# Edge softmax of a graph-attention layer: the row term added to the mask before the turn, on one Trainium2 core

## The chip, the cores and the metric

The kernel runs on one core of one Trainium2 chip. The metric is the device time of one execution in microseconds. The engines are called by the names that the profile uses: PE is TensorE (matrix products; PEld is its weight load), DVE is VectorE, ACT is ScalarE, POOL is GpSimd, SP is SyncE, which issues most of the transfers.

## The reference, cut to what matters

There are 128 graphs of 128 nodes with 512 features each. Two layers follow each other; both have the form "layer norm of x plus a graph layer of x". The first layer is masked attention with 8 heads. The second, which the change touches, is a graph attention with one head:

```python
Wh = h @ W                              # [128 graphs, 128 nodes, 512]
s_i = Wh @ a1 ; s_j = Wh @ a2           # one number for each node
e = leaky(s_i[:, :, None] + s_j[:, None, :])      # leaky(x) = x if x >= 0 else 0.2 x
e = where(adj > 0, e, -9e15)
attention = softmax(e, axis=1)          # over i
h_prime = leaky(einsum('bij,bjf->bif', attention, Wh))
```

The softmax runs over i, the first index, and the product sums over j. So the kernel wants the scores as [j, i]: j on the partitions, i along the free axis, where a reduction can run. The mask comes from memory as adj[i, j], with i on the partitions, the other way round. Something has to be turned.

## The kernel before, in words

All 128 graphs go through one core. The main loop runs over t, one graph a round; a round holds the pieces of several graphs at different stages. Graph t has its attention scores and its softmax (class Softmax); a pair of graphs around t - 3 has the output projection of the first layer (LayerZero); a pair around t - 6 has the product with W of the second layer (LayerOne), and graph t - 7 has the edge softmax (class Edge). The query, key and value projections are made for groups of four graphs and are cut into steps that the rounds consume. Hence the loop has a period of four rounds. Large products are made with seven block products in place of eight (Strassen's scheme); their partial results lie in PSUM banks named st_y, st_w, st_x (projections) and p_y, p_w, p_x (pairs of graphs), and ScalarE and VectorE copy or add them out.

The order of the instructions on every engine is written out by hand: no scheduler moves them. In the loop it is the order of the statements of the body. The last rounds, from END = 124 on, are not a loop but a list of pieces, PLAN (from L1151), in which e0 to e10 are the edge softmaxes of the last eleven graphs; e4.turn is the method turn of the fourth after e0, and so on. The list is walked once and each piece is issued in its turn on its engines.

The names and lines that matter:

- mask_float (L479) turns the loaded adj into bf16 (tile mf, nine buffers), and mask (L484) makes it 0 where there is an edge and -1e30 where there is none. The same tile serves the first layer's softmax and, some rounds later, the edge softmax.
- WH[b] is the result of LayerOne: 2 x 257 columns. Column 256 of the first half holds s_i, column 256 of the second half holds s_j, because the weights w1 have been given that column at the start.
- Edge.turn (L781) makes two products on TensorE into one bank, p_e. L784 turns the column s_i, spread over 128 columns, so that it stands as a row on all partitions; L785 multiplies the mask by a bf16 identity, which turns the mask.
- Edge.add (L794) adds s_j, a bias of each partition, on ScalarE and leaves PSUM (tile e).
- Edge.maxima (L798) makes the leaky ReLU on VectorE (L800), adds the turned mask from the bank (L802), and reduces to the negative maximum (L804).
- Edge.exp, divide, product, copy and residual follow: exponential on ScalarE (L808), division on VectorE (L812, L813), the product with Wh on TensorE (L818, bank p_h), the copy to tile z on ScalarE (L824), and then leaky ReLU, residual and layer norm.

In the loop the turn stands in the early part of a round, after the scores of graph t and one step of the projections, and the product with its copy stands at the end of the round, before the first layer's product with the values (L588, bank p_oT) and its copies (L602). In the loop ScalarE's and VectorE's instructions for the edge softmax lie between the exponentials (L540) and the divisions (L554) of the first layer's softmax. In the tail the layer norm of a graph ends with an activation (L649), and the bias bo is put into the banks p_y and p_w by ScalarE (L456).

The PSUM pool "mm" has five banks, which lg, p_y, p_w, p_x, p_e, p_h and p_oT use one after the other.

Of the kernel before, what the change touches and what calls it, by code (L numbers as in the profile page):

```python
# [9 lines left out]
BF16 = mybir.dt.bfloat16  # L10
I32 = mybir.dt.int32
AF = mybir.ActivationFunctionType
ALU = mybir.AluOpType
# [6 lines left out]
ALPHA = 0.2  # L20
# [4 lines left out]
def kernel(  # L25
# [69 lines left out]
    small = ctx.enter_context(tc.tile_pool(name="small", bufs=3))  # L95
# [4 lines left out]
    def psum(name):  # L100
        return ps_mm.tile([P, D], F32, name=name, tag="mm")


    ident = const.tile([P, P], F32, name="ident")
    make_identity(nc, ident)
    ident_b = const.tile([P, P], BF16, name="ident_b")
    nc.vector.tensor_copy(ident_b, ident)
    mhalf = const.tile([P, 1], F32, name="mhalf")
    nc.gpsimd.memset(mhalf, -0.5)

# [109 lines left out]
    X, XT, XS, Q, K, V, MF, OT, X1T, X1, WH = ({} for _ in range(11))  # L220
# [266 lines left out]
    class Softmax:  # L487
# [45 lines left out]
        def maxima(self):  # L533
            self.add(0)
            self.add(1)
            self.reduce()
# [231 lines left out]
    class Edge:  # L768
# [8 lines left out]
        def tile(self, name, shape, pool, bufs):  # L777
            home = self.homes.get(name)
            return home(shape) if home else pool.tile(shape, F32, name=name, bufs=bufs)

        def turn(self):  # L781
            self.s = WH[self.b][:, :, HALF : HALF + 1]
            self.p = psum("p_e").rearrange("p (c k) -> p c k", c=NC)
            nc.tensor.transpose(self.p[:, 0, :], self.s[:, 0, :].to_broadcast([P, P]), ident)  # L784
            nc.tensor.matmul(  # L785
                self.p[:, 1, :],
                MF.pop(self.b),
                ident_b,
                start=False,
                stop=True,  # L790
                skip_group_check=True,
            )

        def add(self):  # L794
            self.e = self.tile("e", [P, P], small, 1)
            nc.scalar.activation(self.e, self.p[:, 0, :], AF.Identity, bias=self.s[:, 1, :])

        def maxima(self):  # L798
            e = self.e
            nc.vector.scalar_tensor_tensor(e, e, ALPHA, e, op0=ALU.mult, op1=ALU.max)  # L800
            self.att = self.tile("att", [P, P], small, 2)
            nc.vector.tensor_add(self.att, self.p[:, 1, :], e)  # L802
            self.nmax = small.tile([P, 1], F32, name="nmax1", bufs=4)
            nc.vector.tensor_reduce(self.nmax, self.att, AX.X, ALU.max, negate=True)  # L804

# [39 lines left out]
    def on(b):  # L845
        return 0 <= b < B
# [14 lines left out]
    none = Nothing()  # L861
# [7 lines left out]

    zero = {}  # L870
    chores = []
    sm = fin = edge = none

    def x_turns(t):
        if t < 0:
# [58 lines left out]
    END = B - GROUP  # L934
    for t in range(-3, END):
# [29 lines left out]
        last, sm = sm, Softmax(t) if on(t) else none  # L965
# [6 lines left out]
        if t < 3:  # L972
            sm.maxima()
            group(2)
            if on(t - 2):
                load_residual(t - 2)
            if t == 0 and on(GROUP):
                sum_x(1)()
            sm.exp(0, 1, 2, 3)
            last.transpose()  # L980
            group()
            sm.reciprocals(0)
            sm.exp(4, 5, 6, 7)
            sm.reciprocals(1)
            sm.divide(0, 1, 2)
            group()
            last.attend()
            sm.divide(3, 4)
            last.copy()
            if t % 2 == 0 and t > 0:  # L990
                last.sum(0, 1, 2, 3)
            sm.divide(5, 6, 7)
            if on(t + 1):
                mask_float(t + 1)
        else:
            sm.maxima()
            group()
            edge = Edge(t - 7) if on(t - 7) else none
            edge.turn()
            edge.add()  # L1000
            fin.residual()
            if on(t - 2):
                load_residual(t - 2)
            edge.maxima()
            fin.stats()
            fin.rstd()
            x1_sums()
# [12 lines left out]
            fin.apply()  # L1020
            fin.store()
            sm.exp(7)
            edge.divide()
            pair()
            sm.reciprocals(1)
            sm.divide(0, 1, 2, 3)
            group()
            sm.divide(4, 5)
            pair()
            sm.divide(6, 7)  # L1030
            if on(t + 1):
                mask_float(t + 1)
            group()
# [8 lines left out]
        if t % 2 == 0 and on(t - 4):  # L1042
# [2 lines left out]
            layer.transpose(1)  # L1045
            sums.append(layer)
        group(21 if t % GROUP == 0 else 1)
        fin = edge
        fin.product()
        fin.copy()  # L1050
# [98 lines left out]
    for n in range(6):  # L1149
# [7 lines left out]
        el.rstd b0.p2 b0.t2 al.transpose.0 s0.divide.0.1 b0.p7 al.sum.0 b0.c11 s0.divide.6.7  # L1157
        b1.p1 al.sum.1 s1.exp.6.7 s0.store al.sum.2 b0.t3 s1.reciprocals.1 s1.exp.0.1 b0.p4
        b0.c22 al.sum.3 s1.divide.4.5 b0.p3 b0.c21 s0.fetch s1.divide.6.7 s2.scores b0.c12 v.t3
        e0.turn s1.exp.2.3 v.c22 v.p4 m2.cast s1.reciprocals.0 e0.add m2.mask s2.add.0  # L1160
        s1.divide.2.3 v.p3 s2.add.1 s1.divide.0.1 b1.t0 s2.reduce s1.store v.c21 b1.p6 el.apply
        v.c12 s2.exp.2.3 el.store s3.scores e0.maxima s2.exp.6.7 s1.fetch sl.attend e0.exp
        s2.exp.4.5 e0.divide e1.turn b1.p5 s0.transpose sl.copy e0.product m3.cast
        s2.reciprocals.1 sl.sum.0 e1.add m3.mask b1.p2 s3.add.0 s2.divide.6.7 sl.sum.1
        s1.transpose s2.divide.4.5 a0.by a0.p1 sl.sum.2 b1.t2 e0.copy sl.sum.3 b1.p7 b1.c11 a0.t0
        s3.add.1 s2.exp.0.1 a0.p6 s3.reduce b1.t3 s0.attend a0.t2 e0.residual s3.exp.0.1 a0.p7
        s3.exp.6.7 a0.bw a0.p5 b1.c22 x2.x a0.t3 s2.reciprocals.0 e1.maxima s3.exp.2.3 a0.p4
        s2.divide.0.1 a0.c22 b1.p3 e1.exp s3.reciprocals.0 s2.divide.2.3 a0.c21 a0.p3 e1.divide
        s3.divide.0.1 s2.store a0.stats.1 e1.product s3.divide.2.3 b1.c12 a0.rstd.1 s3.exp.4.5
        s1.attend e0.stats e1.copy e3.turn s3.reciprocals.1 e0.rstd b1.p4 s0.copy e1.residual  # L1170
        s2.fetch s1.copy a0.p2 e1.stats x3.x s3.divide.6.7 a0.c11 s1.sum.0 a0.c12 s3.divide.4.5
        s1.sum.1 e3.add s3.store a0.stats.0 s1.sum.2 e0.apply a1.by a1.p1 b1.c21 e1.rstd e0.store
        e3.maxima a0.apply.1 e2.turn a1.p2 a1.t0 a0.store.1 s2.transpose e3.exp a0.rstd.0 a1.p6
        e2.add s3.fetch e1.apply e2.maxima a1.bw a1.p5 s1.sum.3 a1.t2 a0.apply.0 e3.divide a1.p7
        e1.store e2.exp a1.c11 a0.fetch.1 s2.attend e2.divide a1.t3 a1.c22 a1.p4 s2.copy
        a0.store.0 s3.transpose a1.p3 a1.c21 a1.stats.1 s3.attend a0.transpose.1 a0.fetch.0
# [2 lines left out]
        a1.rstd.0 x5.x e2.residual b2.p1 a2.t0 a0.sum.0 a1.apply.0 a1.fetch.1 a2.p6 a2.c11  # L1179
        s3.sum.3 b2.t0 e2.stats b2.p5 a0.sum.1 a2.t2 e3.stats x4.x a0.sum.2 a2.p7 a1.store.0  # L1180
        a0.sum.3 b2.p6 a2.t3 e2.rstd a2.c22 a2.p4 b2.t2 a1.transpose.1 a2.p3 e3.rstd e2.apply
        a1.fetch.0 a2.c21 b2.p7 a2.stats.1 e3.apply e4.turn a2.c12 a2.rstd.1 b2.p2 e2.store
        b2.t3 e3.store e4.add b2.p4 a2.stats.0 a2.apply.1 b2.c22 a2.rstd.0 b2.c21 a2.store.1
        b2.c11 b2.p3 a1.transpose.0 e6.turn e4.maxima a2.apply.0 a1.sum.0 b3.p1 e6.add
        a2.store.0 a1.sum.1 b2.c12 b3.p2 e4.exp e6.maxima b3.t0 a2.fetch.1 a1.sum.2 e5.turn
# [5 lines left out]
        e5.stats e8.turn e6.store e7.turn b4.t3 e8.add b4.p4 b4.c22 e5.rstd e7.add e8.maxima  # L1191
        b4.p3 b4.c21 e7.maxima e8.exp e10.turn e5.apply b4.c12 e7.exp e5.store e8.divide
        e9.turn e10.add e7.divide e8.product e9.add e10.maxima e7.product e8.copy e9.maxima
# [48 lines left out]
```

## Time and profile before

| | |
|---|---|
| time, median of 3 runs | 2434.93 us (2433.65 to 2435.12) |
| the profiled run | 2433.28 us, span 2431.4 us |
| granted TensorE clock, mean | 0.995 of full speed |
| turn of s_i, L784 | 128 of 274 ns, weight load 137 ns |
| product of the mask, L785 | 128 of 219 ns, weight load 99 ns |
| add of s_j on ScalarE, L796 | 128 of 369 ns |
| leaky ReLU L800, add of the mask L802, maximum L804 on VectorE | 128 each, of 284, 292 and 286 ns |
| bytes moved | 379.91 MB, 156 GB/s |

How to read it: a duration runs from an instruction's start to its end[...]. On TensorE and ScalarE the next instruction starts before the one ahead has ended, so the durations of a row can't be added up to a time; the distance from one start to the next tells what an instruction costs its engine. The share of busy time is an average over the whole span, over stages with different limits.

### The profile page before, as it was taken

Reading aid. Unit: us, or ns where it says so; the run is one execution under the profiler, and the core shown is the slowest. Engines: PE = TensorE matmul, PEld = TensorE weight load, DVE = VectorE, ACT = ScalarE, POOL = GpSimd, SP = SyncE. Lnnn points to the kernel's source line nnn. Section 1 sums busy time; section 2 is a strip of 40 time slices with the busy share of each in tenths; the row PEclk is TensorE's granted clock in tenths of the full one; section 3 lists DMA queues with packets and bytes.
Section 4 is the critical chain, followed back from the end, with each engine's and each line's share of the span. In section 5 each row is a group of like instructions: output and inputs, shape, how many; then the busy total and the mean of one; then the engine's idle time right before and its main releaser. Section 6 shows DMA issues by size and latency. Waiting matters only on the chain.

```text
span 2431.4 us, 43517 instructions
## 1 busy us (share of the span) xinstructions
PE 2389.4 (98%) x13585; PEld 1997.9 (82%) x13585; DVE 1840.9 (76%) x3731; ACT 1488.7 (61%) x5334; POOL 805.8 (33%) x1195
## 2 busy tenths in 40 slices
PE   8899999999999999999999999999999999999997
PEld 6688888888888888888888888888888888888874
DVE  5667777777877877777778778778777777787787
ACT  3556566666666665666666566666666665666684
POOL 2123333333332332333333333333333333332335
PEclk9899999999999999999999999999999999999999
DMA  6544545445445445445445454454454454544443
GB/s 192 178 132 149 172 150 159 163 144 165 158 149 169 151 148 168 152 155 168 144 159 161 146 173 144 152 170 150 156 168 140 159 167 148 169 155 143 156 157 107
DMA packets 351111, 379.91 MB, mean 156 GB/s; under 512 B 38936, under 2 KB 255008, under 8 KB 350880
## 3 DMA queue, kind: packets, MB, share of 16 engines
q1 hardware_dynamic: 350016, 376.07, 48.3%
q8 instruction: 109, 1.79, 0.3%
q10 hardware_dynamic: 864, 1.05, 0.2%
q14 instruction: 122, 1.00, 0.1%
HBM read 240.91 MB, written 136.05 MB: 155 GB/s over the span
## 4 chain that ended last, share of the span: by engine, by line
PE 91%; DVE 2%; DMA 2%; issue 2%; ACT 2%; POOL 1%; SPq 1%; DVEq 0%; POOLq 0%; ACTq 0%
PE st_y L354 26%; PE p_y L435 17%; PE st_w L354 13%; PE p_w L435 9%; PE st_x L354 6%; PE lg L506 5%; PE p_oT L588 5%; PE p_x L435 4%; PE p_h L818 4%; DMA wv_n<-wv 1%; DMA pa_dram<-pa 1%; PE p_e L784 1%; ACT pa L554 1%; SPq L228 0%; ACT pa L540 0%
## 5 line engine op out<-in xcount | busy, mean ns | idle before, releaser
L540 ACT ACTIVATE pa<-pa,nmax 128x128 f32<-128x128 f32 x1008 | 392.4, 392 | 11.0 <-DVE nmax L529 5.2
L638 POOL TENSOR_SCALAR ve<-mv 128x1 f32<-128x1 f32 x256 | 69.5, 272 | 896.6 <-DVE mv L634 889.2
L554 ACT ACTIVATE pa<-pa,rs 128x128 f32<-128x128 f32 x1008 | 331.2, 395 | 34.1 <-DVE rs L550 30.5
L520 DVE TENSOR_TENSOR pa<-lg,mf 128x512 f32<-128x512 f32 x252 | 162.0, 685 | 163.3 <-PE lg L506 158.0
L263 POOL TENSOR_TENSOR oS<-oT 128x256 f32<-128x256 f32 x63 | 45.8, 728 | 642.8 <-ACT oT L602 642.8
L331 ACT COPY st_t<-st_y 128x512 f32<-128x512 f32 x192 | 110.4, 575 | 145.3 <-PE st_y L354 142.1
L540 ACT ACTIVATION_READ_ACCUMULATOR pa<-pa,nmax 128x1 f32 x1008 | 191.4, 190 | 0.0
L588 PEld LDWEIGHTS p_oT<-paT,v 128*64 128x64 f32 x2016 | 108.2, 137 | 96.3 <-issue 90.7
L335 ACT ACTIVATE st_t<-st_y,b_cols 128x256 f32<-128x256 f32 x192 | 80.7, 471 | 169.4 <-PE st_y L354 169.4
L640 POOL TENSOR_TENSOR rstd<-ve,mhalf 128x1 f32<-128x1 f32 x256 | 176.5, 690 | 21.3
L602 ACT ACTIVATE oT<-p_oT,b_cols 128x128 f32<-128x128 f32 x504 | 144.0, 368 | 62.4 <-PE p_oT L588 48.2
L446 ACT COPY pr_t<-p_y 128x257 f32<-128x257 f32 (+1 forms) x375 | 137.5, 367 | 48.7 <-PE p_y L435 48.7
L575 DVE STREAM_TRANSPOSE paT<-paz 128x1024 f32<-128x1024 f32 x126 | 156.8, 1245 | 3.4 <-DMA paz<-pa_dram 1.9
L529 DVE TENSOR_REDUCE nmax<-pa 128x8 f32<-128x1024 f32 x126 | 153.7, 1220 | 4.4
L506 PE MATMUL lg<-kT,qT 64*128 64x128 f32 x2048 | 148.7, 285 | 0.0
L588 PE MATMUL p_oT<-paT,v 128*64 128x128 f32 x2016 | 138.8, 280 | 4.7 <-DVE paT L575 4.7
L506 PEld LDWEIGHTS lg<-kT,qT 64*128 64x128 f32 x2048 | 124.2, 187 | 23.2 <-issue 23.2
L435 PE MATMUL p_y<-w,x1T 128*128 128x257 f32 x496 | 131.6, 387 | 1.6 <-ACT wk L446 1.5
L435 PE MATMUL p_y<-wo,oT 128*128 128x256 f32 x504 | 132.9, 386 | 0.2 <-ACT p_y L456 0.2
L435 PE MATMUL p_y<-wo,oS 128*128 128x256 f32 x504 | 129.4, 379 | 0.0
L354 PE MATMUL st_y<-wv_n,xS 128*128 128x256 f32 x512 | 122.1, 382 | 6.3 <-DMA wv_n<-wv 6.2
L435 PE MATMUL p_y<-w,x1S 128*128 128x257 f32 x496 | 128.0, 380 | 0.0
(200 smaller groups left out, 5986.1 us busy)
## 6 DMA issues: line engine op xcount, KB each, us to landing
pa_dram<-pa SPq DMA_DIRECT2D x126, 512.0 KB, 2.6
paz<-pa_dram SPq DMA_DIRECT2D x504, 128.0 KB, 2.6
wv_n<-wv SPq DMA_DIRECT2D x224, 256.0 KB, 2.9
x<-in_x_dram SPq DMA_DIRECT2D x128, 256.0 KB, 3.0
x_dram<-x SPq DMA_DIRECT2D x128, 256.0 KB, 2.5
xz<-x_dram SPq DMA_DIRECT2D x512, 64.0 KB, 2.0
xz<-in_x_dram SPq DMA_DIRECT2D x496, 64.0 KB, 2.2
out_dram<-z SPq DMA_DIRECT2D x120, 256.0 KB, 2.4
```

The source lines that it names most:

```text
L354: nc.tensor.matmul(p[:, m, :], lhs, rhs, start=start and m == 0 and kc == 0, stop=True, skip_group_check=True,)
L435: nc.tensor.matmul(p[:, :width], xs()[n][:, kc, :], w[:, PLACE[n], kc, :], start=start and kc == 0, stop=True, skip_group_check=True,)
L446: nc.scalar.copy(t[:, :width], p[:, :width])
L506: nc.tensor.matmul(self.lg[r][:, c, :], q[rows, c, cols], k[rows, c, cols], start=c == 0, stop=True, skip_group_check=True,)
L520: nc.vector.tensor_add(by_head[:, r * NC : (r + 1) * NC], self.lg[r].rearrange("p c (b k) -> p c b k", b=4), mf.unsqueeze(1).to_broadcast( ...
L529: nc.vector.tensor_reduce(self.nmax, by_head, AX.XY, ALU.max, negate=True)
L540: nc.scalar.activation(self.pa[:, :, h, :], self.pa[:, :, h, :], AF.Exp, bias=self.nmax[:, h : h + 1], accum_out=self.sums[:, h : h + 1],)
L554: nc.scalar.activation(self.pa[:, :, h, :], self.pa[:, :, h, :], AF.Copy, scale=self.rs[:, h : h + 1])
L575: nc.vector.transpose(self.paT.rearrange("p h (a i) -> p a h i", i=32), self.paz.rearrange("p a (h k) -> p a h k", k=32),)
L588: nc.tensor.matmul(self.oT[r * HD : (r + 1) * HD, c, :], v[:, h * HD : (h + 1) * HD], self.paT[:, r * NC + c, :], start=c == 0, stop=True, ...
L602: nc.scalar.activation(OT[pair][:, c, h * P : (h + 1) * P], self.oT[:, c, :], AF.Identity, bias=b_cols[:, 1, c : c + 1],)
L640: nc.gpsimd.tensor_tensor(self.r, ve, mhalf, ALU.pow)
```

## The change

The scores are now built the other way round. Before the turn, ScalarE adds s_i to the mask while both still stand as [i, j] with i on the partitions: one activation, s_i as the bias of each partition, from the bf16 mask to an fp32 tile e (new method sender). TensorE turns this sum once. ScalarE adds s_j to what comes out, as before. The leaky ReLU is applied to the sum with the mask in it, and writes att directly; the separate add of the mask on VectorE, the mask's own product and the bf16 identity are gone. Where there is no edge the value is now 0.2 x (-1e30) in place of -1e30.

In the loop, the new activation is issued at the end of the round before the one that holds the turn, ahead of that round's product and copy (L1048). The object of the edge is made there and is handed to the next round. In PLAN, each eN.turn gets an eN.sender directly in front of it.

```diff
-    ident_b = const.tile([P, P], BF16, name="ident_b")
-    nc.vector.tensor_copy(ident_b, ident)
...
+        def sender(self):
+
+            self.s = WH[self.b][:, :, HALF : HALF + 1]
+            self.e = self.tile("e", [P, P], small, 1)
+            nc.scalar.activation(self.e, MF.pop(self.b), AF.Identity, bias=self.s[:, 0, :])
+
         def turn(self):
-            self.s = WH[self.b][:, :, HALF : HALF + 1]
-            self.p = psum("p_e").rearrange("p (c k) -> p c k", c=NC)
-            nc.tensor.transpose(self.p[:, 0, :], self.s[:, 0, :].to_broadcast([P, P]), ident)
-            nc.tensor.matmul(
-                self.p[:, 1, :],
-                MF.pop(self.b),
-                ident_b,
-                start=False,
-                stop=True,
-                skip_group_check=True,
-            )
+            self.p = psum("p_e")[:, :P]
+            nc.tensor.transpose(self.p, self.e, ident)
 
         def add(self):
-            self.e = self.tile("e", [P, P], small, 1)
-            nc.scalar.activation(self.e, self.p[:, 0, :], AF.Identity, bias=self.s[:, 1, :])
+            nc.scalar.activation(self.e, self.p, AF.Identity, bias=self.s[:, 1, :])
 
         def maxima(self):
             e = self.e
-            nc.vector.scalar_tensor_tensor(e, e, ALPHA, e, op0=ALU.mult, op1=ALU.max)
             self.att = self.tile("att", [P, P], small, 2)
-            nc.vector.tensor_add(self.att, self.p[:, 1, :], e)
+            nc.vector.scalar_tensor_tensor(self.att, e, ALPHA, e, op0=ALU.mult, op1=ALU.max)
...
-            edge = Edge(t - 7) if on(t - 7) else none
+            edge = coming
             edge.turn()
...
         group(21 if t % GROUP == 0 else 1)
+        coming = Edge(t - 6) if on(t - 6) and t + 1 < END else none
+        coming.sender()
         fin = edge
         fin.product()
...
-        e0.turn s1.exp.2.3 v.c22 v.p4 m2.cast s1.reciprocals.0 e0.add m2.mask s2.add.0
+        e0.sender e0.turn s1.exp.2.3 v.c22 v.p4 m2.cast s1.reciprocals.0 e0.add m2.mask s2.add.0
```

The other ten turns of PLAN get their sender in the same way.

More of the change, by code (lines that the diff above doesn't have):

```diff
@@ L871 @@
     chores = []
-    sm = fin = edge = none
+    sm = fin = edge = coming = none
     def x_turns(t):
@@ L1159 @@
         b0.c22 al.sum.3 s1.divide.4.5 b0.p3 b0.c21 s0.fetch s1.divide.6.7 s2.scores b0.c12 v.t3
-        e0.turn s1.exp.2.3 v.c22 v.p4 m2.cast s1.reciprocals.0 e0.add m2.mask s2.add.0
+        e0.sender e0.turn s1.exp.2.3 v.c22 v.p4 m2.cast s1.reciprocals.0 e0.add m2.mask s2.add.0
         s1.divide.2.3 v.p3 s2.add.1 s1.divide.0.1 b1.t0 s2.reduce s1.store v.c21 b1.p6 el.apply
         v.c12 s2.exp.2.3 el.store s3.scores e0.maxima s2.exp.6.7 s1.fetch sl.attend e0.exp
-        s2.exp.4.5 e0.divide e1.turn b1.p5 s0.transpose sl.copy e0.product m3.cast
+        s2.exp.4.5 e0.divide e1.sender e1.turn b1.p5 s0.transpose sl.copy e0.product m3.cast
         s2.reciprocals.1 sl.sum.0 e1.add m3.mask b1.p2 s3.add.0 s2.divide.6.7 sl.sum.1
@@ L1169 @@
         s3.divide.0.1 s2.store a0.stats.1 e1.product s3.divide.2.3 b1.c12 a0.rstd.1 s3.exp.4.5
-        s1.attend e0.stats e1.copy e3.turn s3.reciprocals.1 e0.rstd b1.p4 s0.copy e1.residual
+        s1.attend e0.stats e1.copy e3.sender e3.turn s3.reciprocals.1 e0.rstd b1.p4 s0.copy e1.residual
         s2.fetch s1.copy a0.p2 e1.stats x3.x s3.divide.6.7 a0.c11 s1.sum.0 a0.c12 s3.divide.4.5
         s1.sum.1 e3.add s3.store a0.stats.0 s1.sum.2 e0.apply a1.by a1.p1 b1.c21 e1.rstd e0.store
-        e3.maxima a0.apply.1 e2.turn a1.p2 a1.t0 a0.store.1 s2.transpose e3.exp a0.rstd.0 a1.p6
+        e3.maxima a0.apply.1 e2.sender e2.turn a1.p2 a1.t0 a0.store.1 s2.transpose e3.exp a0.rstd.0 a1.p6
         e2.add s3.fetch e1.apply e2.maxima a1.bw a1.p5 s1.sum.3 a1.t2 a0.apply.0 e3.divide a1.p7
@@ L1181 @@
         a0.sum.3 b2.p6 a2.t3 e2.rstd a2.c22 a2.p4 b2.t2 a1.transpose.1 a2.p3 e3.rstd e2.apply
-        a1.fetch.0 a2.c21 b2.p7 a2.stats.1 e3.apply e4.turn a2.c12 a2.rstd.1 b2.p2 e2.store
+        a1.fetch.0 a2.c21 b2.p7 a2.stats.1 e3.apply e4.sender e4.turn a2.c12 a2.rstd.1 b2.p2 e2.store
         b2.t3 e3.store e4.add b2.p4 a2.stats.0 a2.apply.1 b2.c22 a2.rstd.0 b2.c21 a2.store.1
-        b2.c11 b2.p3 a1.transpose.0 e6.turn e4.maxima a2.apply.0 a1.sum.0 b3.p1 e6.add
-        a2.store.0 a1.sum.1 b2.c12 b3.p2 e4.exp e6.maxima b3.t0 a2.fetch.1 a1.sum.2 e5.turn
+        b2.c11 b2.p3 a1.transpose.0 e6.sender e6.turn e4.maxima a2.apply.0 a1.sum.0 b3.p1 e6.add
+        a2.store.0 a1.sum.1 b2.c12 b3.p2 e4.exp e6.maxima b3.t0 a2.fetch.1 a1.sum.2 e5.sender e5.turn
         b3.p6 e4.divide a1.sum.3 e5.add e6.exp e5.maxima e4.product b3.t2 a2.fetch.0 e6.divide
@@ L1190 @@
         e6.stats a2.sum.3 b4.p6 b3.c12 e6.rstd b4.c11 b4.p5 b4.t2 e5.residual b4.p7 e6.apply
-        e5.stats e8.turn e6.store e7.turn b4.t3 e8.add b4.p4 b4.c22 e5.rstd e7.add e8.maxima
-        b4.p3 b4.c21 e7.maxima e8.exp e10.turn e5.apply b4.c12 e7.exp e5.store e8.divide
-        e9.turn e10.add e7.divide e8.product e9.add e10.maxima e7.product e8.copy e9.maxima
+        e5.stats e8.sender e8.turn e6.store e7.sender e7.turn b4.t3 e8.add b4.p4 b4.c22 e5.rstd e7.add e8.maxima
+        b4.p3 b4.c21 e7.maxima e8.exp e10.sender e10.turn e5.apply b4.c12 e7.exp e5.store e8.divide
+        e9.sender e9.turn e10.add e7.divide e8.product e9.add e10.maxima e7.product e8.copy e9.maxima
         e10.exp e7.copy e8.residual e9.exp e8.stats e10.divide e8.rstd e9.divide e10.product
```

## The prediction, before the changed kernel was run

> **What bounds the kernel now.** I read the page's busy shares first, then the waits, then the chain of waits, and then TensorE's timeline around the lines that the change touches. Columns of the waits: who waited, for what, us in total, times, longest. The first fence is the page's part 1; the second is the answer for the waits of TensorE between 150 and 2310 us, and the third the same from 2310 us to the end.
>
> ```profile
> PE 2389.4 (98%) x13585; PEld 1997.9 (82%) x13585; DVE 1840.9 (76%) x3731; ACT 1488.7 (61%) x5334; POOL 805.8 (33%) x1195
> ```
>
> ```profile
> PE st_y L354 <- DMA wv_n<-wv: 0.3, 1, 0.3
> ```
>
> ```profile
> PE p_h L818 <- DVE rt L812: 3.2, 1, 3.2
> PE p_y L435 <- ACT p_y L456: 2.2, 2, 2.0
> PE p_y L435 <- ACT wk L446: 1.5, 2, 1.0
> PE p_w L435 <- DVE wh L759: 1.0, 1, 1.0
> ...
> ```
>
> In 2160 us of the loop TensorE waits 0.3 us in all. It is not merely busy, it is the only limit there; all other engines wait for it (ScalarE alone 99.2 us, 58 times, at its e <- p_e). Only in the tail, after 2345 us, is there a mixed chain of waits. So an edit in the loop is worth what it takes out of TensorE's spacing. Here is that spacing (timeline: start, length, engine, line, operation); lengths overlap, so I use starts.
>
> ```profile
> 1198.46 0.27 PE L784 MATMUL p_e<-ident,wh 128*128 128x128 f32 x1
> 1198.57 0.22 PE L785 MATMUL p_e<-ident_b,mf 128*128 128x128 bf16 x1
> 1198.62 1.08 PE L435 MATMUL p_y<-wo,oT 128*128 128x256 f32 x4
> 1199.54 1.03 PE L435 MATMUL p_w<-wo,oS 128*128 128x256 f32 x4
> ```
>
> From the turn to p_w pass 1.08 us. The same group of four elsewhere takes 0.864 us (1203.00 to 1203.86), here 0.92: the bf16 product of the mask costs its own slot, 0.055, and about the same again in the group behind it, whose first weight load does not fit behind a slot of 0.055.
>
> **What the Trainium skill says.** "TensorE: Matmul & The Clock Gate", section Back-to-back issue gap, gives N/2.4 + 2.5 ns, 56 ns for 128 bf16 columns; the trace has 55. Its section LDWEIGHTS gives columns/1.2, 107 ns for 128 columns; the trace has fp32 weight loads starting 110 ns apart at their closest. Both together explain the 0.92: a load of 110 behind a slot of 55 sticks out by 55. "ScalarE: Activation LUTs", section Step-by-step, says that bias and scale are free and that fp32 and bf16 elements pass at the same rate; so the added activation costs what its neighbours cost. No run here has that operation on a bf16 source yet.
>
> **The change, part by part.**
>
> *Mask product removed (L785), per edge.* After the turn (spacing 0.109, as before) the group starts at once; its first load, 0.110, fits behind 0.109 to within a few ns. Turn to p_w becomes 0.109 + 4 x 0.216 = 0.973 instead of 1.084: 0.111 us saved. Bounds: 0.055 if the load sticks out after all, 0.112 if nothing does. I take 0.111. The turn itself now moves a real fp32 tile instead of a broadcast column; the nearest row, the p_x turns of L906, also has fp32 tiles 0.109 apart, so no change. Its weight load lies behind a 0.216 slot.
>
> *The loop:* 117 edges x 0.111 = 13.0 us less on the only limit. The remaining 11 edges are in the written-out tail, where I count by hand below.
>
> *New activation e <- mf + s_i on ScalarE.* By the neighbours its occupancy is 0.29 (starts of the L554 activations are 0.292 apart; L540 and L554 last 0.39; L602, which reads PSUM, follows at 0.25): bounds 0.25 to 0.39, taken 0.29, 128 x 0.29 = 37 us on an engine that is 61% busy. Where does it lie? It stands at the end of a round, in front of z <- p_h. The four rounds of a period leave ScalarE 0.27, 0.27, 2.0 and 0.01 us idle in front of that copy, and about 0.5 behind it. The tightest round:
>
> ```profile
> 1249.74 0.84 ACT L335 ACTIVATE st_t<-st_y,b_cols 128x256 f32<-128x256 f32 x2 [3.59 <-PE st_y L354]
> 1250.59 0.59 ACT L824 COPY z<-p_h 128x512 f32<-128x512 f32 x1
> 1251.69 1.14 ACT L602 ACTIVATE oT<-p_oT,b_cols 128x128 f32<-128x128 f32 x4 [0.51 <-PE p_oT L588]
> ```
>
> Even here z moves to 1250.9 and is over before the oT copies, which wait for TensorE until 1251.69. So the rest of ScalarE's queue does not move; z is read by VectorE only in the next round.
>
> *New wait: the turn now waits for ScalarE.* Behind the turn stand all of TensorE's products of the round. The instruction ahead of the new activation ends 3.85 to 5.84 us before the turn in every loop round; less 0.4 for the activation, over 3.4 us are left. TensorE's sequencer meets the semaphore 2.6 us ahead of the turn (it met L784's at 1195.88), still after it is set. The new activation needs no wait of its own in the loop: mask and s_i are older than waits that ScalarE has already made.
>
> *VectorE:* the add L802 goes, 128 x 0.29 = 37 us, and with it a wait between two of its own instructions. It does not limit the loop; in the tail it helps. The bf16 identity goes: one copy of some 0.3 us at the start, beside the first loads. *Buffers and queues:* the bank of p_e comes free at ScalarE's add instead of VectorE's, some 2.5 us earlier in the round above; the mask's buffer earlier too. No DMA and no GpSimd instruction is added or moved on SP's or POOL's queue.
>
> **The tail, 11 edges.** There the activation stands directly in front of its turn, so TensorE waits for whatever ScalarE has queued. I moved each one by hand through the timeline (times of before):
> - e0, e3: ScalarE is just done when TensorE arrives (2342.6, 2363.3): no stall. e1: 0.2 late, swallowed by the wait for p_y L456 at 2352.6.
> - e3 pushes the bias copy L456 by 0.25, for which TensorE waits 2.0 at 2367.5: +0.25. e2 adds 0.25, but the next wait there (p_w L456, 2371.1) hangs on VectorE's maxima, which come 0.3 earlier: back to about -0.2.
> - e4 is the largest:
>
> ```profile
> 2389.90 0.27 PE L784 MATMUL p_e<-ident,wh 128*128 128x128 f32 x1
> ...
> 2391.01 0.81 ACT L649 ACTIVATE wq<-wq,shift,rstd 128x512 f32<-128x512 f32 x1 [1.22 <-POOL shift L645]
> ...
> 2391.73 0.35 ACT L446 COPY wk<-p_y 128x257 f32<-128x257 f32 x1
> ...
> 2392.14 1.14 PE L435 MATMUL p_y<-w,x1T 128*128 128x257 f32 x4 [0.99 <-ACT wk L446]
> ```
>
> The activation stands behind L649 of 2391.01, so the turn slips from 2389.90 to about 2392.1. TensorE was to lose 0.99 at 2392.14 anyway, with 0.87 of work between: +0.8 net.
> - e6, e5 +0.1 each, mostly taken back by 2407, where TensorE waits 0.99 for VectorE: about +0.4 left. e8, e7 stand behind L649 of 2408.79: +0.5. e10, e9 stand behind it and two exponentials: e8's product slips from 2413.0 to 2414.6, but VectorE's queue, which carries the end, waited for two maxima until 2415.26, and gets them 0.3 shorter each: +1.0 at the end.
>
> Sum: -13.0 + 1.0 = -12.0 us on a span of 2431.4. Bounds for the tail: -1.3 (its 11 products saved, nothing given back) to +3 (each late turn paid in full). The span is of the profiled run, 2433.28 by the clock; the three timed runs lie at 2433.65 to 2435.12. I take the same 12.0 from the median 2434.93: 2422.9.
>
> **Rivals.**
> 1. *Half the saving:* the group's first weight load still sticks out behind the turn. For: the load's 0.110 and the slot's 0.109 are equal to a few ns. Against: 109 ns spacing of the p_x turns, each with its own load. 128 x 0.055 = 7, less 1 in the tail: 2428.9.
> 2. *Hidden anyway:* something just behind TensorE, ScalarE's copies out of the product banks, takes over. For: the shortest time between such a copy and the next product into p_y is 0.43 in nearly all rounds. Against: that is four times 0.11, and ScalarE waits for TensorE in every round. No change: 2434 to 2435.
> 3. *Slower:* the new activation lies on TensorE's path, because the turn waits for it in the loop too. It decides from 0.111 per edge; if its 0.29 were paid in full, 128 x (0.29 - 0.111) = +23: 2458. For: the tail, where this happens. Against: over 3.4 us of lead in every loop round; the lead would have to vanish entirely.
> 4. *The change does not do what it says:* against this, the instruction orders of both kernels differ by 128 mask loads and products less on TensorE, 128 adds less on VectorE, 128 activations more on ScalarE and the identity's copy, and nothing else.
>
> **How the numbers follow.** Forecast 0.83, rival 1 0.07, rival 2 0.05, rival 3 0.04, other 0.01 (counted as faster). A measurement of this kernel tells about 0.2%, 4.9 us, from no change. Forecast and rival 1 are faster by more: 0.91; same 0.05; slower 0.04. The forecast's own range is 2420 to 2426 (tail bounds, run spread 0.7 either way); stretched toward rival 1 and a tail that behaves better or worse than traced: 2419.5 to 2428.0.
>
> **What would show it.** In the changed profile: turn (p_e) to p_w 0.97 us; a round pair of the loop shorter by 0.22; TensorE's loop waits still near 0.3 us; the new activation at 0.39 with 0.29 spacing, mostly in idle time; 37 us more on ScalarE, 37 less on VectorE, 28 less in TensorE's busy sum (which overlaps); waits of the turn for ScalarE in the tail alone, the largest near e4 with some 2 us. I am wrong if TensorE waits for the new activation in the loop, if turn to p_w stays above 1.0, or if the tail from 2310 us is longer by more than 3.

## The result, and the profile after

The changed kernel takes **2423.46 us** (median of 4 runs, 2421.84 to 2425.66); the kernel before took 2434.29 us on the same chip (median of 4, 2431.71 to 2435.12). The ratio is 0.9958, with a 95% interval of 0.9941 to 0.9975. The profiled run of the changed kernel is the longest of its four: 2425.66 us, span 2423.8.

The same views as before, in the same order. First the page's part 1:

```profile
PE 2378.0 (98%) x13457; PEld 1986.4 (82%) x13457; DVE 1810.4 (75%) x3602; ACT 1520.8 (63%) x5462; POOL 800.0 (33%) x1195
```

128 instructions fewer on TensorE, 129 fewer on VectorE, 128 more on ScalarE. Next, TensorE's waits, between 150 and 2310 us and then from 2290 us to the end (who waited, for what, us in total, times, longest):

```profile
PE st_y L353 <- DMA wv_n<-wv: 1.1, 1, 1.1
```

```profile
PE p_e L788 <- ACT wk L784: 4.9, 4, 2.4
PE p_h L812 <- DVE rt L806: 2.7, 1, 2.7
PE p_y L434 <- ACT p_y L455: 2.4, 1, 2.4
```

In the loop TensorE still waits for a single transfer only, and never for the new activation (tile e). In the tail the new activation (there its tile is a part of wk) is the largest wait, 4.9 us in four turns. Now the timeline of TensorE around the turn, with its columns of start, length, engine, line and operation:

```profile
1193.53 0.27 PE L788 MATMUL p_e<-ident,e 128*128 128x128 f32 x1
1193.63 1.03 PE L434 MATMUL p_y<-wo,oT 128*128 128x256 f32 x4
1194.50 1.03 PE L434 MATMUL p_w<-wo,oS 128*128 128x256 f32 x4
```

From the turn to p_w pass 0.97 us (1194.50 - 1193.53) where it was 1.08: the mask's slot is gone, and the group of four is back to 0.87. Last, ScalarE in the round that the prediction called the tightest:

```profile
1244.47 0.84 ACT L334 ACTIVATE st_t<-st_y,b_cols 128x256 f32<-128x256 f32 x2 [3.59 <-PE st_y L353]
1245.20 0.40 ACT L784 ACTIVATE e<-mf,wh 128x128 f32<-128x128 bf16 x1
1245.49 0.58 ACT L818 COPY z<-p_h 128x512 f32<-128x512 f32 x1
1246.42 1.14 ACT L601 ACTIVATE oT<-p_oT,b_cols 128x128 f32<-128x128 f32 x4 [0.35 <-PE p_oT L587]
```

The new activation takes 0.29 of ScalarE (1245.20 to 1245.49) and pushes the copy z; the copies oT, which wait for TensorE, start 1.95 us after L334, as they did before (1249.74 to 1251.69). It lies in idle time.

To place the difference I cut each trace at turns, by their starts: the loop runs from the first to the 117th turn, the tail from the 117th turn to the end of the span, and a period is the most frequent distance over four rounds.

| | period | loop | tail | median, and ratio to before on the same chip |
|---|---|---|---|---|
| before | 74.08 | 2149.3 | 121.6 | 2434.29 |
| changed | 73.64 | 2137.3 | 125.4 | 2423.46; 0.9958 [0.9941, 0.9975] |
| difference | -0.44 | -12.0 | +3.7 | -10.8 |

The loop gained 12.0, the tail gave 3.7 back, and the stretch ahead of the first turn is 0.7 longer, which makes the 7.6 between the two spans. The medians lie 10.8 apart; the profiled run of the changed kernel has a piece of the tail, told below, that not every execution has.

### The profile page after: what moved, and what is told of

It is laid out like the page before. It is cut to its first block, busy times and chain, and to the rows that moved or that the text cites. A ratio compares the mean times of both kernels' runs of the same rounds, so it can differ in the third digit from the quotient of the medians.

```text
span 2423.8 us, 43195 instructions
## 1 busy us (share of the span) xinstructions
PE 2378.0 (98%) x13457; PEld 1986.4 (82%) x13457; DVE 1810.4 (75%) x3602; ACT 1520.8 (63%) x5462; POOL 800.0 (33%) x1195
## 4 chain that ended last, share of the span: by engine, by line
PE 92%; ACT 2%; DVE 2%; DMA 2%; issue 1%; POOL 1%; SPq 0%; ACTq 0%; DVEq 0%; POOLq 0%
PE st_y L353 26%; PE p_y L434 17%; PE st_w L353 13%; PE p_w L434 9%; PE st_x L353 7%; PE lg L505 5%; PE p_oT L587 5%; PE p_x L434 4%; PE p_h L812 4%; PE p_e L788 1%; ACT pa L539 1%; ACT pa L553 0%; DMA wv_n<-wv 0%; DMA pa_dram<-pa 0%; POOL rstd L639 0%
## 5 line engine op out<-in xcount | busy, mean ns | idle before, releaser
L334 ACT ACTIVATE st_t<-st_y,b_cols 128x256 f32<-128x256 f32 x192 | 80.5, 470 | 170.5 <-PE st_y L353 170.5
L505 PEld LDWEIGHTS lg<-kT,qT 64*128 64x128 f32 x2048 | 124.2, 187 | 23.2 <-issue 22.9
```

What stands on the lines that cost most here:

```text
L505: nc.tensor.matmul(self.lg[r][:, c, :], q[rows, c, cols], k[rows, c, cols], start=c == 0, stop=True, skip_group_check=True,)
```

## The experiments

Two theories. **A:** the loop's gain is TensorE's slot of the mask product and nothing else, the activation is free there, and what the tail gives back comes from turns that wait for ScalarE. **B:** the gain comes from the lighter load on VectorE (the add of the mask gone), or the activation costs something in the loop too and the real saving is larger. All kernels below but the last two ran in two groups, each group on one chip with the kernel before.

### The changed kernel again (after_again)

No edit.

> The changed kernel once more, on the chip of the next three. Theory (13.0 us won in the loop, some 3.7 us given back in the tail, as its first profile shows): 9 to 12 us below the kernel before. The stretch after the wait for p_y L455 near 2357 us ran at a granted clock of 0.57 in the first profile; if that is chance it is at 1.00 here and the tail is about 1.1 us shorter.

Measured: 2424.9 us against 2436.68, ratio 0.9951 [0.9938, 0.9963]; period 73.64, loop 2136.7, tail 124.2. The loop's gain repeats to within a us; the tail is 1.2 shorter than in the first trace. The difference begins at one spot. In the first trace, shortly behind TensorE's wait of 2.4 us for p_y L455, which ends at 2356.26, its timeline reads:

```profile
2357.83 1.92 PE L434 MATMUL p_x<-wo,spare 128*128 128x256 f32 x4
2359.54 1.59 PE L434 MATMUL p_y<-wo,spare 128*128 128x256 f32 x4
2360.96 1.03 PE L434 MATMUL p_w<-wo,spare 128*128 128x256 f32 x4
```

The first two groups of four take 1.71 and 1.42 from start to start where 0.87 is usual: about seven products stand 427 ns apart in place of 216. The view by stretches (stretch, length, busy PE, PEld, VectorE, ScalarE, GpSimd with counts, granted clock, DMA share, GB/s) shows that nothing was waited for; the clock was lower:

```profile
2356.20:2360.20 4.00, 3.79 (x11) 2.87 (x12) 3.38 (x9) 3.25 (x10) 3.36 (x10) 0.63 0.86 312
```

This dip costs TensorE about 1.5 us (7 x 0.21), and this tail is 1.2 longer than that of after_again; the trace of before has no dip. So tails are compared below with a note on it; the cleanest pair is before (121.6) against after_again (124.2): **+2.6**.

### The mask product put back beside the new form (mask_back)

Theory A says that all of the loop's gain must go, though VectorE keeps its lighter load.

```diff
-            nc.scalar.activation(self.e, MF.pop(self.b), AF.Identity, bias=self.s[:, 0, :])
+            self.m = MF.pop(self.b)
+            nc.scalar.activation(self.e, self.m, AF.Identity, bias=self.s[:, 0, :])
...
-            self.p = psum("p_e")[:, :P]
+            bank = psum("p_e")
+            self.p = bank[:, :P]
             nc.tensor.transpose(self.p, self.e, ident)
+            nc.tensor.matmul(
+                bank[:, P : 2 * P],
+                self.m,
+                ident_b,
...
```

The product's result lies in further columns of the bank, which nobody reads.

> The changed kernel with a bf16 product of the mask by the identity put back behind each turn, into columns that nobody reads. Theory (the gain is TensorE's slot of 0.055 plus the 0.056 by which the next weight load sticks out): the loop's spacing is that of the kernel before again, 74.08 us for four rounds, and the time is 12 to 14 us above the changed kernel, within 4 us of the kernel before. Rival (the gain comes from VectorE's missing add, or from the bank that comes free earlier): both are still there, so it stays 10 us or more below the kernel before.

Measured: 2438.87 us, ratio to before 1.001 [1.0001, 1.0018]; period 74.08, as before; tail 126.0, with the dip. Its timeline:

```profile
1198.63 0.27 PE L792 MATMUL p_e<-ident,e 128*128 128x128 f32 x1
1198.74 0.22 PE L793 MATMUL p_e<-ident_b,mf 128*128 128x128 bf16 x1
1198.79 1.08 PE L436 MATMUL p_y<-wo,oT 128*128 128x256 f32 x4
1199.71 0.59 PE L436 MATMUL p_w<-wo,oS 128*128 128x256 f32 x2
```

1.08 again. The whole gain of the loop is this product, 0.11 us for an instruction whose own slot is 0.055 (1198.74 to 1198.79). This speaks against B: VectorE's lighter load and the activation are both in this kernel, and the period is that of before to the hundredth.

### The gain without the activation (vector_alone)

The kernel before, with the mask product written onto the turned s_i in the bank, so that the sum is made there. ScalarE has no new work, TensorE keeps the mask product, VectorE loses its add.

```diff
             nc.tensor.matmul(
-                self.p[:, 1, :],
+                self.p[:, 0, :],
                 MF.pop(self.b),
...
-            nc.vector.scalar_tensor_tensor(e, e, ALPHA, e, op0=ALU.mult, op1=ALU.max)
             self.att = self.tile("att", [P, P], small, 2)
-            nc.vector.tensor_add(self.att, self.p[:, 1, :], e)
+            nc.vector.scalar_tensor_tensor(self.att, e, ALPHA, e, op0=ALU.mult, op1=ALU.max)
```

> The kernel before with VectorE's part of the change alone: the mask's product adds onto the turned s_i in the bank, ScalarE adds s_j to the sum, and the leaky ReLU comes last; no activation and no TensorE product is added or removed. Theory (VectorE does not limit the loop): four rounds take 74.08 us as before, VectorE is busy 37 us less, and the time is 0 to 1.5 us below the kernel before, won in the tail. Rival (VectorE's add was on a path that ends in TensorE): 4 us or more below it.

Measured: 2432.43 against 2435.2, ratio 0.9989 [0.9983, 0.9996]; period 74.08, tail 120.8. Part 1 of its page:

```profile
PE 2390.1 (98%) x13585; PEld 1998.3 (82%) x13585; DVE 1807.0 (74%) x3603; ACT 1490.7 (61%) x5334; POOL 813.2 (33%) x1195
```

VectorE is 34 us lighter than before and the loop's period is not a hundredth shorter. In the tail it is worth 0.9. The medians differ by 2.8, more than expected; of that the profiles show the 0.9, and I did not find the rest.

### The activation twice (double)

```diff
-            nc.scalar.activation(self.e, MF.pop(self.b), AF.Identity, bias=self.s[:, 0, :])
+            m = MF.pop(self.b)
+            nc.scalar.activation(self.e, m, AF.Identity, bias=self.s[:, 0, :])
+            if not self.on_scalar:
+                twice = small.tile([P, P], F32, name="twice", bufs=1)
+                nc.scalar.activation(twice, m, AF.Identity, bias=self.s[:, 0, :])
```

In the loop alone, the same activation is made a second time, into a tile that nobody reads.

> The changed kernel with the added activation issued twice in the loop, the second time into a tile that nobody reads. Theory (it lies in ScalarE's idle time around the copy of z, 0.3 to 2.0 us in front of it and 0.5 behind): four rounds still take 73.64 us, and the time is within 2 us of the changed kernel, though ScalarE is busy 35 us longer. Rival (a part of the activation is on the path, so that more than 0.11 per edge was won and some given back): up to 117 x 0.3 = 35 us above it, and four rounds longer than 73.64.

Measured: 2421.38, ratio 0.9941 [0.9929, 0.9954]; period 73.64, tail 124.0. The row of the second activation (mean ns: smallest, median, largest; then first and last start):

```profile
L788 ACT ACTIVATE twice<-mf,wh x117: 388/390/399, 154.3 to 2289.3; 128x128 f32<-128x128 bf16 x117
```

ScalarE is busy 1550.8 us, 30 longer, with 117 more instructions, and TensorE waits for none of them. The loop has room for twice the activation.

### The activation too late (late)

The prediction's third rival needs the lead of the activation to vanish. Here it does: the sender stands directly in front of its turn in the loop too.

```diff
-            edge = coming
+            edge = Edge(t - 7) if on(t - 7) else none
+            edge.sender()
             edge.turn()
...
-        coming = Edge(t - 6) if on(t - 6) and t + 1 < END else none
-        coming.sender()
```

> The changed kernel with the loop's added activation moved from the end of the round before to directly in front of its turn; the tail stays. Theory (the early place carries the change: in two of four rounds ScalarE stands at a copy of a product bank that ends after TensorE has come to the turn): those two turns wait about 1.4 and 1.1 us, the other two not; four rounds take 73.64 + 2.5 = 76.2 us, and the time is about 75 us above the changed kernel, near 2498. Rival (the turn's place does not matter since ScalarE is only 63% busy): within 2 us of the changed kernel.

Measured: 2498.61 against 2435.2, ratio 1.026 [1.0244, 1.0276]; period 76.28, loop 2213.3. TensorE's waits in the loop, and one of them in its timeline (in brackets the idle time ahead of the instruction and what ended it):

```profile
PE p_e L788 <- ACT e L784: 61.5, 56, 1.2
```

```profile
1265.19 0.33 PE L788 MATMUL p_e<-ident,e 128*128 128x128 f32 x1 [1.22 <-ACT e L784]
```

The period grows by 2.64 over that of the changed kernel, where four activations occupy 4 x 0.29 = 1.2. So what is paid when the producer comes late is not its own duration alone, but also the queue ahead of it on ScalarE: the wait of 1.22 us shown begins at 1263.97, and the activation, behind a copy out of a product bank, starts only at 1264.74 and lasts 0.40. Rival 3 is real, and the placement one round ahead is what keeps it away: the same instructions, in another place, turn -11 us into +63.

### The eleven tail edges in their old form (tail_before)

```diff
+    class OldEdge(Edge):
+        def sender(self):
+            pass
...
-        jobs[f"e{n}"] = Edge(
+        jobs[f"e{n}"] = OldEdge(
```

The methods turn, add and maxima of OldEdge are those of the kernel before.

> The changed kernel in the loop, the kernel before in the eleven edges of the tail. Theory (the tail's turns wait for ScalarE): TensorE's waits for the added activation are gone, from the 117th turn to the end it takes the 119.5 us of the kernel before, and the time is 2.5 to 4 us below the changed kernel. Rival (the tail's loss was a dip of the clock or scatter between runs): within 1 us of the changed kernel.

Measured: 2419.99, ratio 0.9938 [0.9925, 0.9952]; period 73.64, tail 122.1 without the dip. It keeps the loop's gain, and all its positions in the tail stay within 0.4 of before. So, as traced, taking the old form back removes 2.1 of the 2.6 us (124.2 - 122.1); about 1 of these 2.1 is a wait for a transfer that, as shown further down, did not come with the new form alone. In the medians this kernel is 4.9 us below the changed one, more than the 2.5 to 4 expected. The 119.5 us of the expectation is not the 121.6 that this way of cutting gives for before; against that, this tail is 0.4 longer. Among TensorE's waits from 2290 us there is none of a turn any more; the largest is p_h's for VectorE, 3.9 in two.

### The senders of the tail earlier in the list (early)

If lateness is the cost, it should go when each sender stands earlier on ScalarE. In the list, e2.sender moves behind e0.copy, e3.sender behind b1.t3, e4.sender behind a2.by, e7.sender and e8.sender behind e4.apply, e9.sender behind b4.c11. One of the lines:

```diff
-        a1.fetch.0 a2.c21 b2.p7 a2.stats.1 e3.apply e4.sender e4.turn a2.c12 a2.rstd.1 b2.p2 e2.store
+        a1.fetch.0 a2.c21 b2.p7 a2.stats.1 e3.apply e4.turn a2.c12 a2.rstd.1 b2.p2 e2.store
```

> The changed kernel with six of the eleven activations of the tail (e2, e3, e4, e7, e8, e9) moved to earlier places in the list, where ScalarE idles for TensorE or GpSimd. Theory: e4's wait of 2.4 us and that of 1.15 us at e8 disappear, e10's and part of e9's stay; TensorE keeps the saved products, so 3 to 5 us below the changed kernel and 0 to 1.5 us below the one with the old tail. Rival (what VectorE and GpSimd do in the tail sets the end, not the turns): within 1 us of the changed kernel.

Measured: 2423.57, ratio 0.9942 [0.9929, 0.9954]; tail 122.6, with the dip. TensorE's waits from 2290 us:

```profile
PE p_h L812 <- DVE wk L807: 2.9, 2, 2.6
...
PE p_e L788 <- ACT wk L784: 0.3, 1, 0.3
```

The waits for the activation fall from 4.9 to 0.3, as theory A has it, and the traced tail is 1.6 shorter than that of after_again although it pays the dip. In the median it is only 1.3 below the changed kernel, less than I expected. The dip's 1.5 us is of the same size, and which of the timed runs had it is not recorded, so the medians don't decide between the theory and its rival.

### Both kinds of edge (mixed), and the sum made in the bank (tail_summed)

mixed: the changed loop; e0 to e3 and e10 in the old form, the others new, with the senders of e4, e7, e8 and e9 placed as in early. tail_summed: the changed loop, and all tail edges in the form of vector_alone. It ran on another chip, beside a third run of the changed kernel (after_third).

```diff
-        jobs[f"e{n}"] = Edge(
+        jobs[f"e{n}"] = (OldEdge if n < 4 or n == 10 else Edge)(
```

> The changed loop; in the tail e0 to e3 and e10 as in the kernel before, and e4, e7, e8, e9 with the activation at earlier places (behind a2.by, e4.apply and b4.c11), e5 and e6 as changed. Theory (where ScalarE is full, the added activation costs; where it idles, it is free): from the 117th turn to the end about 121.1 us, so 0 to 1 us below the one with the old tail (122.06) and 3 to 5 below the changed kernel; TensorE's wait for p_y L455 stays at 2.4 us or less between starts, and no dip of the clock follows. Rival: the tail is as long as with the old turns, 121.6 to 122.1.

> The changed loop; in the eleven edges of the tail no added activation, the mask's product added onto the turned s_i in the bank, leaky ReLU last. Theory (TensorE is short in the loop, ScalarE and VectorE in the tail): from the 117th turn to the end 120.8 us as in the kernel with VectorE's part alone, the loop at 73.64 us for four rounds; 3 to 5 us below the changed kernel and about 1 us below the one with the old tail, near 2419. Rival (the shorter tail of that kernel was chance): 121.6 to 122.1 us as with the old tail.

> The changed kernel on the same chip, for the comparison: 9 to 12 us below the kernel before; the tail 124.2 us, or 125.4 if the clock dips after the wait for p_y L455.

| | period | tail | median and ratio to before |
|---|---|---|---|
| mixed | 73.64 | 121.7 | 2419.7; 0.9934 [0.9921, 0.9946] |
| tail_summed | 73.64 | 122.2, with the dip | 2422.37; 0.9932 [0.9918, 0.9945] |
| after_third | 73.65 | 125.6, with the dip | 2426.62; 0.9955 [0.9943, 0.9968] |

tail_summed lies 4.2 below after_third on the same chip; its tail missed the 120.8 that I expected by 1.4, which is about what the dip costs. mixed's 121.7 misses the 121.1 that I expected and lies in its rival's range, so the mix of forms is not shown to be better than the old form alone. The three best kernels, tail_before, mixed and tail_summed, have ratios of 0.9932 to 0.9938 whose intervals overlap nearly whole: all three beat the kernel before by 15 to 17 us, and tail_before and tail_summed, which ran beside the changed kernel, beat that by 4.9 and 4.2; they are not told apart.

## Why the prediction was right, and where it was not

**The limit and the saving per edge: right.** Turn to p_w was to be 0.973 and is 0.975 to 0.982; the period is 0.44 shorter (4 x 0.111). Both terms of the explanation hold, the slot of 0.055 and the weight load that stuck out behind it: mask_back brings back 0.11, not 0.055. The traces also show where the second term lies: in all 117 rounds the first two products of the group that follows start 0.27 us apart in before and in mask_back, and 0.22 in the changed kernel, where 0.216 is usual. So rival 1 is out, and the figures of "TensorE: Matmul & The Clock Gate" (sections Back-to-back issue gap and LDWEIGHTS) agree with what was removed.

**The loop's sum:** -13.0 predicted, -12.0, -12.7 and -11.7 in the three traces of the changed kernel. The periods give 29 x 0.44 = 12.8; what is missing are single waits for the transfer wv_n, as in the 1.1 above against 0.3 before.

**The activation hidden: right**, by double (room for a second one) and by late (what it costs where it is not hidden, so rival 3 was a question of place). Its lead is shorter than the "over 3.4 us" of the forecast in one round, the first: it ends 2.95 us ahead of the turn there, and 3.57 to 5.54 us in the others. Its length is 0.397 to 0.407 and its occupancy, where the next instruction follows at once, 0.29. "ScalarE: Activation LUTs", section What ACT_TABLE_LOAD costs, puts an activation with a per-partition bias at about 280 ns + 0.833 per element, 387 ns for 128, with 93 ns of overlap back to back: 294. The trace has that, with a bf16 source too. The 280 ns include some 93 for the per-partition operand, so by this section the bias is not free in time, as the prediction took it to be from another section of the same page. No run here leaves the operand out. The forecast's 0.29 did not rest on it, for it was read off neighbours that carry such an operand themselves.

**Rival 2, hidden anyway: out**, for the period is shorter; and so is theory B, by vector_alone.

**Busy sums:** ScalarE +32 (37 predicted), VectorE -30 (37). Busy time is a union, and neighbours overlap. TensorE -11 and not -28: my 128 x 0.219 counted the full length of an instruction whose neighbours cover most of it. The span was not built on these.

**The tail: the late turns right, the size wrong.** The term "+1.0 at the end" measured +2.6 (after_again against before, both without the dip). By positions behind the 117th turn:

| step | predicted | before | after_again | difference |
|---|---|---|---|---|
| p_y behind the bias copy, e3 | +0.25 | 57.73 | 57.85 | +0.1 |
| e2's turn | +0.5 | 58.70 | 59.14 | +0.4 |
| p_w behind it | -0.2 | 61.34 | 61.06 | -0.3 |
| e4's turn | +2.2 | 80.12 | 82.11 | +2.0 |
| the p_y behind e4's turn and its work | +0.8 | 82.36 | 83.14 | +0.8 |
| e6's turn, and e5's | +0.1 more each | 84.20 | 85.07 | +0.9 |
| p_x, which reads x1T | mostly taken back | 92.70 | 94.39 | **+1.7** |
| p_w where VectorE is awaited | +0.4 | 97.33 | 98.86 | **+1.5** |
| e8's turn | +0.5 more | 99.17 | 102.01 | +2.8 |
| end of the span | +1.0 | 121.64 | 124.21 | **+2.6** |

Everything to e5 is within 0.2 of the hand count. Two later terms of the sum were too small in this trace: at p_w, where the prediction has "mostly taken back by 2407 ... about +0.4 left", +1.5 is left, and "e8, e7: +0.5" became +0.9. TensorE's waits in the first trace of the changed kernel, at e4 and at the last late turns:

```profile
2382.19 0.33 PE L788 MATMUL p_e<-ident,wk 128*128 128x128 f32 x1 [2.38 <-ACT wk L784]
...
2401.62 0.62 PE L788 MATMUL p_e<-ident,wk 128*128 128x128 f32 x2 [1.15 <-ACT wk L784]
...
2405.83 0.33 PE L788 MATMUL p_e<-ident,wk 128*128 128x128 f32 x1 [1.05 <-ACT wk L784]
```

Behind the first of the two stands a wait of p_x, 1.0 us in after_again, for x1T, which VectorE turns out of xz. A layer norm's activation on ScalarE (a2.apply.0, L648 on x) makes x, which is stored to memory and fetched again in another layout, as xz, in eight transfers. VectorE at this turn, before and in after_again:

```profile
2401.54 1.30 DVE L233 STREAM_TRANSPOSE x1T<-xz 128x512 f32<-128x512 f32 x2
```

```profile
2391.01 1.31 DVE L232 STREAM_TRANSPOSE x1T<-xz 128x512 f32<-128x512 f32 x2 [1.43 <-DMA xz<-x_dram]
```

The late turn of e4 does reach this chain: the copy of the product behind it comes later, e6's new activation stands behind that copy, and a2.apply.0 behind both. In after_again ScalarE reads:

```profile
2381.60 0.38 ACT L756 COPY wh<-p_y 128x257 f32<-128x257 f32 x1 [0.67 <-PE p_y L434]
2382.01 0.40 ACT L784 ACTIVATE wk<-mf,wh 128x128 f32<-128x128 bf16 x1
2382.31 0.80 ACT L648 ACTIVATE x<-x,shift,rstd 128x512 f32<-128x512 f32 x1
```

But this delay is only 0.6 us: a2.apply.0 starts 84.92 us behind the 117th turn where it was 84.28, and the last fetch is issued at 89.63 where it was 89.00. Before, that fetch landed at 90.97 and VectorE came to it at 91.76, so there were 0.8 us of slack for these 0.6. What is longer as well is the time from issue to landing. Here are the last three fetches in the view of the transfers (how many, KB each, median us to landing), before and then in after_again, there with one more line, of queue q8 (packets, MB, share):

```profile
xz<-x_dram SPq DMA_DIRECT2D x3, 64.0 KB, 2.0
```

```profile
q8 instruction: 1, 0.02, 2.3%
xz<-x_dram SPq DMA_DIRECT2D x3, 64.0 KB, 3.5
```

One packet of 16 KB, of a kind that the profile calls "instruction", is under way in after_again from 89.82 to 91.26. Nine of the 12 profiles have such a packet while these eight fetches are under way, and in each of the nine a fetch takes 3.0 us or more; before, vector_alone and late have none, and there none takes over 2.2 (the traces have the landing of six of the eight). The form of the tail's edges does not decide it: tail_before has the old form and the packet, and fetches of up to 3.5 us; late has the changed kernel's own tail, a wait of 2.1 us at e4, no packet, and no wait of p_x. From e4's turn to the end late takes 41.05 us, and the four other traces with that tail (changed, after_again, double, after_third) take 41.55 to 42.10.

So about 1 us of the +2.6 goes with this packet and not with the late turns. From e4's turn to the p_w of the table late takes 15.7 us, where before takes 17.2 and after_again 16.8; behind e4's +2.0 this would leave +0.5 at p_w, close to the +0.4 of the prediction. That is an estimate from these traces. No run moved the packet or a2.apply.0 alone, and whether the change had a part in when the packet comes stays open.

The second term does not hang on the packet: e8's turn comes 1.3 us further behind, with 1.15 of waiting for two activations that stand behind L648, and the product behind the turns, which before had waited 0.5 there anyway, 0.9. From there to the end another 0.2 are added, 0.1 in the prediction. The prediction bounded the tail by +3, which holds without the dip and not with it (+3.7).

**The total** stood within 0.6 us of the forecast, 2423.46 against 2422.9; that closeness is partly luck. In the traces the loop gains 11.7 to 12.7, 0.3 to 1.3 less than counted, and the tail costs 1.6 more than counted without the dip and 2.7 more with it, and the medians' scatter of some 3 us hides both: the differences of the medians are 10.8, 11.8 and 10.4 in the three runs of the changed kernel, against 12.0.

## What to carry to other kernels

Price an instruction by the start-to-start distance it takes out of the limiting engine, its effect on the neighbour's weight load included: here a 0.055 us slot was worth 0.11. When work moves to an engine with room, what decides is where the producer stands in that engine's queue: one round ahead it was free, directly in front of its reader the period grew by 2.64 us. And where a delayed instruction is followed by hand, follow what queues behind it too, to the transfers it releases, and compare the delay with the slack there before blaming it: here 0.6 us of delay met 0.8 of slack, and the wait came from transfers that landed late. In a hand-written tail, where the engine that takes over the work has its own queue, it can pay to leave the old form in place: up to 2.1 us in the traces here.

## What the runs showed of the hardware that was not expected

**The dip of the clock.** After TensorE's wait of 2.0 to 2.4 us for the bias copy of p_y in the tail, about seven products ran at half their rate (427 ns apart and not 216) in 6 of the 12 profiles: changed, after_third, mask_back, early, late, tail_summed. Before, after_again, double, mixed, tail_before and vector_alone have the same wait and no dip. The traces show what decides: where the wait falls. In each trace the granted clock changes only on a grid of steps of 3.41 us, and the dip is one such step at half clock. In the six profiles with the dip, the step ahead of it holds at least 2.02 us of TensorE's idle time; in the other six a border of the grid cuts the wait in two, and no step holds more than 1.94. Two steps of the changed kernel, and then two of before (columns as in the view by stretches above):

```profile
2353.84:2357.25 3.41, 1.02 (x5) 0.68 (x4) 3.15 (x9) 3.41 (x10) 3.16 (x6) 1.00 0.86 298
2357.25:2360.66 3.41, 3.26 (x9) 2.56 (x9) 2.40 (x6) 2.20 (x7) 2.82 (x8) 0.50 0.84 284
```

```profile
2363.56:2366.97 3.41, 1.93 (x10) 1.37 (x8) 3.13 (x7) 3.41 (x12) 3.10 (x7) 1.00 0.79 227
2366.97:2370.39 3.42, 2.88 (x14) 2.35 (x14) 3.21 (x8) 2.92 (x9) 2.94 (x7) 1.00 0.84 322
```

The rest of the 12 traces agrees: of all steps at full clock, the 46 that were followed by half clock have TensorE busy for 1.39 us or less, and the 8360 that were followed by full clock for 1.47 or more. "TensorE: Matmul & The Clock Gate", section What's actually happening, says that the clock falls to half after an idle window of about 3.4 us and that this window runs free of the program, so that the same kernel can meet it differently from run to run. The half rate, the length of the window and the changing outcome agree with that; but the window need not be idle throughout, for here 2.0 us of idle time within it were enough. So neither form of the kernel is the cause of the dip: a wait of this length meets it or not by where it falls in the grid. The wait is 2.0 us long in before and 2.4 in the changed kernel, so more positions should suffice for the changed one; the 12 profiles are too few to count that.

**The transfers that land late.** The same "instruction" packets come some 108 times in every trace. Over all 12 traces the 502 fetches of xz from x_dram that have such a packet under way beside them land 3.0 us after their issue in the median, the 4094 others 2.0. That the packet holds them up is inferred from this going together; no run here took the packets away.
